# Attention decoder kernel: where a bias table is built, where a weight load is issued and where one projection group stands in the first block

## The chip, the cores and the metric

The kernel runs on one core of a Trainium2 chip. The metric is device time in microseconds (us) for one launch, the median of three runs; before the change it is 2969.03 us (2966.66 to 2971.7). All arithmetic is float32[...].

## The reference, cut to what matters

The program is one encoder layer on a short context (2 sequences of 77 rows), followed by one decoder layer on a long sequence (2 x 2048 rows, width 512, 16 heads of 32). The part that the change touches is the decoder's causal self-attention and, beside it, the encoder that is worked through in its gaps.

```python
def _rel_bias(emb, qlen, klen):
    rp = k - q
    bucket = jnp.where(rp < 0, jnp.minimum(-rp, MD - 1), jnp.minimum(rp, MD - 1) + MD)
    return emb[bucket].transpose(2, 0, 1)

# decoder, D = 512, H = 16, MD = 128, Tt = 2048
sb = _rel_bias(dec_rel_self, Tt, Tt) + causal[None]
yn = _ln(y, dec_n1_s, dec_n1_b)
y = y + _mha(yn, yn, dec_sa_in_w, dec_sa_in_b, dec_sa_out_w, dec_sa_out_b, sb)
y = y + _mha(_ln(y, ...), memory, ..., cb)      # cross-attention to the encoder's output
y = y + relu(ln(y) @ ff1 + b) @ ff2 + b
```

Scores are scaled by 1/sqrt(32), the bias is added, softmax is taken over the keys at or before the query.

## The kernel before, in words

The decoder's rows are cut into 8 blocks of 512 rows (2 sequences x 4), and a block into 4 row tiles t of 128. Heads are taken in 4 groups g of 4. A **unit** is one (block, group, row tile): 128 units in all, 16 in each block. The order of everything is written out by hand: `slot(n)` runs before unit n's turn of work, first the functions in `light[n]`, then the projection jobs in `jobs[n]`. Around a slot, `scores` writes q times k into PSUM and its copies with bias and maximum go to VectorE (L362 without bias, L369 with it, L376 the maximum), `exps` runs the exponentials on ScalarE (L379), `turn` transposes probabilities on TensorE (L403) and copies them out (L407 VectorE, L409 ScalarE), `values` multiplies them by v (L420). [...]

**The start (L921 to L960).** Four row tiles of x are loaded, `vecs` (scales and biases) and `rel` (the relative-bias embedding, 16 heads x 255) after them, then the first q and k weights (`wqk`, two buffers in `small_w`, L190) and the v weights (`wbig`, L196). `make_bias(1, rel, v)` (L88 to L94) writes a shifted copy of the self-attention table on VectorE in three instructions (L89 memset, L90 subtract, L93 memset of the causal part) and stores it 32 times into the DRAM tensor `tz` with one DMA (L94). Two rows of biases follow (`bv`, `bo`, L83). `load_bias` (L321) later reads `tz` back with a skew, four DMAs for each group. Then comes a software-pipelined layer norm over the four row tiles: `norm_stats` (L264, L265, L267 on VectorE and a power on GpSimd, L268), `norm_center` (L274) and `norm_turn` (L286 transposes on TensorE, evicted by one VectorE instruction at L293 and three ScalarE instructions at L291), with idle transposes (`warm`, L950) between them on TensorE. The result nT feeds the q and k projections (L206, L217), whose evictions are L208 (VectorE) and L222 (ScalarE).

**The stages of the encoder (L444 to L707)** are put one into each slot (`light[n]`): stage 5 multiplies by v (L529) and loads two more weights, stage 6 computes the scores of the first sequence (L538) and works on them on VectorE (L547 to L549). `light[1]` and `light[6]` also make the encoder's and the cross-attention's bias tables with the same `make_bias`.

**The jobs.** In the first block q and k of group 0 run at slot -1, of group 1 at slots 2 and 3, of group 2 at 4 and 5, of group 3 at 5 and 6. `load_next` issues weight loads ahead of the jobs, in the order of the jobs; it is called before every job and holds at most two small weights in flight, because there are two buffers:

```python
        def load_next():

            while len(loaded) < min(len(queue), ran[0] + (5 if ran[0] < 4 else 3)):
                ahead = [queue[i][2] for i in range(ran[0], len(loaded) + 1)]
                if sum(ahead) > 2:
                    break
                loaded.append(queue[len(loaded)][0]())
```

All DMAs are issued by SyncE's queue (SP), in program order: an issue that waits for a buffer holds up all later ones. TensorE, VectorE and ScalarE also run in program order. The tail of the program (cross-attention and the feed-forward of all blocks, in a form with seven products instead of eight) is not touched by the change, except for its line numbers, which move by up to three.

Of the kernel before, what the change touches and what calls it, by code (L numbers as in the profile page):

```python
# [54 lines left out]
def tile_encoder_decoder(ctx: ExitStack, tc: tile.TileContext, ins, out):  # L55
    nc = tc.nc
    x, src = ins["x"], ins["ctx_1024"]
# [19 lines left out]
    def vec(name, i):  # L77
        c = _COL[name] + i
        return vecs[:, c : c + 1]

    def row_into(t, name):
        i = _ROWS.index(name)
        nc.sync.dma_start(t, ins["rows"][i : i + 1, :].to_broadcast([P, D]))  # L83
# [4 lines left out]
    def make_bias(m, rel, v):  # L88
        nc.vector.memset(v[:, m, :], 0.0)  # L89
        nc.vector.tensor_scalar(v[:, m, P : P + NREL], rel[:, m, :], rel[:, m, 0:1], None, ALU.subtract)  # L90
        if m == 1:

            nc.vector.memset(v[:, m, 2 * P : LT], NEG)  # L93
        nc.sync.dma_start(tz[m][:, :RB, :], v[:, m : m + 1, :].to_broadcast([H, RB, LT]))  # L94
# [54 lines left out]
    with (  # L149
# [20 lines left out]
        def bank():  # L170

            i = count["bank"] % count["banks"]
            count["bank"] += 1
            return psum[:, i, :]
# [13 lines left out]
        def small_w(c0, name="dec_sa_in_wT"):  # L188
            w = sb.tile([P, NC, P], F32, name="wqk", tag="wqk", bufs=2)
            nc.sync.dma_start(w, wchunk(name, c0, P))  # L190
            return w
# [10 lines left out]
        def q_job(b, m, g):  # L202
            def run(w):
                mm = bank()
                for c in range(NC):
                    nc.tensor.matmul(mm, w[:, c, :], nTs[b, m][:, c, :], start=(c == 0), stop=(c == NC - 1))  # L206
                q = sb.tile([P, MB], F32, name="q", tag="q", bufs=3)
                nc.vector.tensor_scalar(q, mm, vec("dec_sa_in_b", g), SCALE, ALU.add, ALU.mult)  # L208
                qTs[b, m, g] = q

            return lambda: small_w(g * P), run, True

        def k_job(b, m, g):
            def run(w):
                mm = bank()
                for c in range(NC):
                    nc.tensor.matmul(mm, w[:, c, :], nTs[b, m][:, c, :], start=(c == 0), stop=(c == NC - 1))  # L217
                d, bi = kT[:, g, ts(m, MB)], vec("dec_sa_in_b", NC + g)
                if m >= 2:
                    nc.vector.tensor_scalar(d, mm, bi, None, ALU.add)  # L220
                else:
                    nc.scalar.activation(d, mm, AF.Identity, bias=bi)  # L222

            return lambda: small_w(D + g * P), run, True

        def v_job(b, m, t):
            def run(w):
                mm = bank()
                for c in range(NC):
                    nc.tensor.matmul(  # L230
                        mm, nTs[b, m][:, c, ts(t, P)], w[:, c, :], start=(c == 0), stop=(c == NC - 1)
                    )
                nc.vector.tensor_tensor(vv[:, m * TB + t, :], mm, bv, ALU.add)

            return lambda: big_w("v", b, m), run, False

        def out_job(b, m, t):
            def run(w):
                x1 = xr.pop((b, m, t))
                mm = bank()  # L240
                for c in range(NC):
                    nc.tensor.matmul(
                        mm, ots[b, m, c][:, ts(t, P)], w[:, c, :], start=(c == 0), stop=(c == NC - 1)
                    )
                nc.vector.tensor_tensor(x1, mm, x1, ALU.add)
                nc.sync.dma_start(y1[b][m][:, t, :], x1)

            return lambda: big_w("o", b, m), run, False

        def residual(b, m, t):  # L250
            x1 = xr[b, m, t] = sb.tile([P, D], F32, name="xr", tag="xr", bufs=2)
            nc.sync.dma_start(x1, x_rows[b, m, :, t, :])
            nc.gpsimd.tensor_tensor(x1, x1, bo, ALU.add)  # L253

        def norm_load(b, m, t, place=None):
            x1 = sb.tile([P, D], F32, name="xt", tag="xt", bufs=2) if place is None else place
            nc.sync.dma_start(x1, x_rows[b, m, :, t, :])
            xs[b, m, t] = x1

        def norm_stats(b, m, t):  # L260
            x1 = xs[b, m, t]
            st = sm.tile([P, 6], F32, name="bnst", tag="bnst")
            mv = sm.tile([P, 2], F32, name="bnmv", tag="bnmv")
            nc.vector.bn_stats(st, x1)  # L264
            nc.vector.bn_aggr(mv, st)  # L265
            rs = sm.tile([P, 2], F32, name="rstd", tag="rstd")
            nc.vector.tensor_scalar_add(rs[:, 0:1], mv[:, 1:2], EPS)  # L267
            nc.gpsimd.tensor_tensor(rs[:, 1:2], rs[:, 0:1], mhalf[:, 0:1], ALU.pow)  # L268
            xs[b, m, t] = x1, mv, rs

        def norm_center(b, m, t):
            x1, mv, rs = xs[b, m, t]
            xs[b, m, t] = x1
            nc.vector.tensor_scalar(x1, x1, mv[:, 0:1], rs[:, 1:2], ALU.subtract, ALU.mult)  # L274
# [608 lines left out]
        jobs = {n: [] for n in range(-1, len(units) + NU)}  # L883
# [4 lines left out]
        for x, (b, m) in enumerate(blocks):  # L888
            u = x * NU
            first = m == 0  # L890

            jobs[u + 1 if first else max(u - 3, -1)].append(v_job(b, m, 0))
            jobs[u + 2 if first else u - 2].append(v_job(b, m, 1))
            jobs[u + 3 if first else u + 1].append(v_job(b, m, 2))
            jobs[u + 4 if first else u + 2].append(v_job(b, m, 3))
            jobs[max(u - 5, -1)].append(q_job(b, m, 0))
            jobs[max(u - 4, -1)].append(k_job(b, m, 0))
            jobs[u - 1 if x else 2].append(q_job(b, m, 1))
            jobs[u if x else 3].append(k_job(b, m, 1))
            for g, at in ((2, 3), (3, 5)) if x else ((2, 4), (3, 5)):  # L900
                jobs[u + at].append(q_job(b, m, g))
                jobs[u + at + 1].append(k_job(b, m, g))
            for t in range(TB):
                end = x == len(blocks) - 1
                jobs[u + NU + (2 if end else 7) + t].append(out_job(b, m, t))
                at = u + NU + ((-1, 0, 3, 4)[t] if end else 6 + t)
                light[at].append(lambda b=b, m=m, t=t: residual(b, m, t))
                if x:
                    light[u - NU + 5 + t].append(lambda b=b, m=m, t=t: norm_load(b, m, t))
                    ahead[u - NU + 6 + t].append(lambda b=b, m=m, t=t: norm_stats(b, m, t))  # L910
                    light[u - NU + 6 + t].append(lambda b=b, m=m, t=t: norm_center(b, m, t))
                    light[u - NU + 7 + t].append(lambda b=b, m=m, t=t: norm_turn(b, m, t))
            for g in range(NC):
                d = divide(b, m, g)
                for k in range(2):
                    light[u + g * TB + TB + k].append(lambda d=d: next(d, None))
                at = u + g * TB - 3
                light[max(at, -1)].append(lambda b=b, m=m, g=g: load_bias(b, m, g))
# [7 lines left out]
        rel = pp[:H, 12288 : 12288 + 3 * NREL].rearrange("h (m u) -> h m u", u=NREL)  # L926
# [4 lines left out]
# [7 lines that stand above are left out]
# [1 line left out]
        ran = [0]  # L939
        load_next()  # L940
        v = pp[:H, 13056 : 13056 + 3 * LT].rearrange("h (m u) -> h m u", u=LT)
        make_bias(1, rel, v)
        row_into(bv, "sa_bv")
        row_into(bo, "dec_sa_out_b")

# [7 lines left out]
        for t in range(TB + 2):  # L953
            if t < TB:
                norm_stats(0, 0, t)
            if 1 <= t <= TB:
                norm_center(0, 0, t - 1)
            if t >= 2:
                norm_turn(0, 0, t - 2, apart=True)
                warm(6)  # L960
# [4 lines left out]
        def slot(n):  # L965
            for f in light[n]:
                f()
            for _, run, _ in jobs[n]:
                load_next()
                run(loaded[ran[0]])  # L970
                ran[0] += 1

        for r, fs in first_cross().items():
            light[len(units) // 2 + 1 + r] += fs
# [253 lines left out]
        turned_to, scored_to, at = {n: 0 for n in range(end)}, {}, [0]  # L1228
# [19 lines left out]
        while i < len(stream):  # L1248
            n = stream[i][0]
# [86 lines left out]
```

## Time and profile before

| | |
|---|---|
| median of 3 runs | 2969.03 us (2966.66 to 2971.7) |
| the profiled execution | 2966.73 us, span 2965.0 us, mean granted TensorE clock 0.986 |
| TensorE matmuls | 2878.4 us busy (97%) |
| VectorE | 2199.0 us busy (74%) |
| ScalarE | 1219.4 us busy (41%) |
| GpSimd | 738.0 us busy (25%) |
| DMA | 137.10 MB, mean 46 GB/s |

The page gives busy time for each engine over the whole span. A busy share of 97% is an average: at single places TensorE waits for a DMA or for VectorE, and those places are found in the waits and in the timeline of a stretch. The view of stretches gives, for each stretch, the busy time of each engine, the granted TensorE clock ("PEclk", 1.00 is full) and the DMA share. In the waits, "A <- B" reads: A stood idle until B.

### The profile page before, as it was taken

The page shows a single profiled execution, that of the slowest core. Times are in us where ns is not written, and L with a number is a line of the kernel's source. Part 1 is how long each engine was busy: PE and PEld are TensorE (multiplying, and loading weights), DVE is VectorE, ACT ScalarE, POOL GpSimd, SP SyncE. Part 2 cuts the span into 40 slices and gives each one's busy share as a digit, 9 for nine tenths or more (in the row PEclk, how much of TensorE's full clock was granted, in tenths as well). Part 3 has the DMA queues.
Part 4 walks back from the last instruction along what each step waited for, and adds up shares of the span by engine and source line. Part 5 has one row for each costly group of instructions (what it writes and reads, how often), then busy time and mean ns, then how long its engine had stood idle before and what let it go on. Part 6 is the DMA issues. An engine that isn't in the chain of part 4 may idle for free. (4 is left out here: it accounts for less than half of the span.)

```text
span 2965.0 us, 60688 instructions
## 1 busy us (share of the span) xinstructions
PE 2878.4 (97%) x24440; PEld 2021.5 (68%) x24440; DVE 2199.0 (74%) x6171; ACT 1219.4 (41%) x2211; POOL 738.0 (25%) x601
## 2 busy tenths in 40 slices
PE   8899999999999999999999997999999899999999
PEld 5456666666666556566666674777777777777788
DVE  4767688878987788788878883767676766766765
ACT  3344456546665455555556671213131313131311
POOL 0100000000000101000000004464646464646465
PEclk9799999999999999999999998999999999999999
DMA  6313301201112403202101224000001000000000
GB/s 174 87 53 116 102 16 51 66 16 44 33 41 70 128 19 87 65 23 63 39 16 37 64 75 136 1 29 1 29 1 38 10 29 1 29 1 29 1 15 15
DMA packets 117644, 137.10 MB, mean 46 GB/s; under 512 B 18241, under 2 KB 73073, under 8 KB 117235
## 3 DMA queue, kind: packets, MB, share of 16 engines
q1 hardware_dynamic: 117362, 133.22, 15.6%
q8 instruction: 192, 3.15, 0.5%
q14 instruction: 90, 0.73, 0.1%
HBM read 111.33 MB, written 21.86 MB: 45 GB/s over the span
## 5 line engine op out<-in xcount | busy, mean ns | idle before, releaser
L379 ACT ACTIVATE pp<-pp,nm 128x128 f32<-128x128 f32 (+15 forms) x512 | 614.0, 1209 | 201.4 <-DVE nm L376 198.8
L362 DVE TENSOR_SCALAR_CACHE_REDUCE pp<-psum 128x512 f32<-128x512 f32 (+3 forms) x1024 | 558.1, 589 | 47.3 <-PE psum L353 45.3
L403 PE MATMUL psum<-ident,pp 128*128 128x128 f32 x4352 | 549.5, 279 | 18.3 <-DVE mx L369 11.8
L403 PEld LDWEIGHTS psum<-ident,pp 128*128 128x128 f32 x4352 | 475.0, 142 | 132.3 <-DVE pp L362 57.1
L409 ACT COPY pts<-psum 128x512 f32<-128x512 f32 (+3 forms) x592 | 298.9, 577 | 510.3 <-PE psum L403 401.0
L1103 POOL TENSOR_TENSOR vv<-pp 128x512 f32<-128x512 f32 x320 | 416.7, 1318 | 148.0 <-PE psum L1120 122.8
L407 DVE COPY pts<-psum 128x512 f32<-128x512 f32 (+2 forms) x544 | 329.9, 660 | 42.0 <-PE psum L403 39.3
L353 PE MATMUL psum<-kT,q 32*128 32x512 f32 (+3 forms) x2560 | 352.0, 580 | 4.8 <-ACT kT L222 1.6
L420 PEld LDWEIGHTS psum<-pts,vv 128*32 128x32 f32 x8704 | 226.2, 110 | 124.0 <-issue 116.9
L420 PE MATMUL psum<-pts,vv 128*32 128x128 f32 x8704 | 278.7, 275 | 0.1
L268 POOL TENSOR_TENSOR rstd<-rstd,mhalf 128x1 f32<-128x1 f32 x32 | 18.2, 568 | 929.6 <-DVE rstd L267 929.6
L1140 ACT ACTIVATE kT<-kT,vecs 128x256 f32<-128x256 f32 x256 | 115.2, 499 | 297.5 <-DVE kT L1137 297.5
L1137 DVE TENSOR_TENSOR kT<-kT,psum 128x512 f32<-128x512 f32 x256 | 166.5, 680 | 86.7 <-PE psum L1120 81.5
L369 DVE CUSTOM_DVE_ANT_0 pp<-psum,bias 128x256 f32<-128x256 f32 (+1 forms) x512 | 209.6, 409 | 21.1 <-PE psum L353 21.1
L353 PEld LDWEIGHTS psum<-kT,q 32*128 32x128 f32 x2560 | 119.5, 184 | 148.5 <-issue 98.5
L1151 PE MATMUL psum<-vv 128*128 128x256 f32 x768 | 176.9, 381 | 0.0
L1120 PE MATMUL psum<-oT,vv 128*128 128x256 f32 x736 | 166.5, 380 | 0.0
L1151 PEld LDWEIGHTS psum<-vv 128*128 128x128 f32 x768 | 143.1, 190 | 26.8 <-issue 9.5
L1120 PEld LDWEIGHTS psum<-oT,vv 128*128 128x128 f32 x736 | 138.8, 190 | 24.4 <-issue 6.2
L1103 DVE TENSOR_TENSOR vv<-kT 128x512 f32<-128x512 f32 x160 | 137.8, 879 | 10.8 <-PE psum L1151 9.9
L253 POOL TENSOR_TENSOR xr<-xr,row_dec_sa_out_b 128x512 f32<-128x512 f32 x32 | 40.6, 1270 | 399.1 <-DMA xr<-in_x_dram 203.7
L206 PE MATMUL psum<-nT,wqk 128*128 128x512 f32 x256 | 120.3, 614 | 3.7 <-DMA wqk<-in_dec_sa_in_wT_dram 3.7
(175 smaller groups left out, 3928.6 us busy)
## 6 DMA issues: line engine op xcount, KB each, us to landing
wqk<-in_dec_sa_in_wT_dram SPq DMA_DIRECT2D x64, 256.0 KB, 3.6
bias<-tz SPq DMA_DIRECT2D x128, 128.0 KB, 3.8
wbig<-in_dec_sa_in_wT_dram SPq DMA_DIRECT2D x8, 1024.0 KB, 7.5
vv<-in_enc_ff_wT_dram SPq DMA_DIRECT2D x8, 1024.0 KB, 5.4
wbig<-in_dec_sa_out_wT_dram SPq DMA_DIRECT2D x8, 1024.0 KB, 7.4
xr<-in_x_dram SPq DMA_DIRECT2D x32, 256.0 KB, 3.3
y<-xr SPq DMA_DIRECT2D x32, 256.0 KB, 2.8
vv<-y SPq DMA_DIRECT2D x32, 256.0 KB, 3.4
```

The costliest lines, as they stand in the source:

```text
L353: nc.tensor.matmul(banks[r][:, : kn * P], q[rows4(r), ts(t, P)], kT[rows4(r), g, k0 * P : (k0 + kn) * P], start=True, stop=True,)
L362: nc.vector.tensor_scalar(p[:, k0 * P : (k0 + far) * P], s[:, : far * P], 1.0, None, ALU.mult, ALU.max, accum_out=st["mx"][:, r, c : c + 1],)
L369: nc.vector.tensor_tensor_reduce(p[:, (i + 1) * P - w : (i + 1) * P], s[:, far * P : kn * P], biases[b, m, g][:, r, 2 * P - w :], 1.0, LOW ...
L379: nc.scalar.activation(p, p, AF.Exp, bias=nm, accum_out=to)
L403: nc.tensor.transpose(pt[:, ts(x, P)], state[n]["p"][r][:, ts(k, P)], ident)
L407: nc.vector.tensor_copy(pts[:, : len(load), :], pt[:, :w])
L409: nc.scalar.copy(pts[:, : len(load), :], pt[:, :w])
L420: nc.tensor.matmul(ot[rows4(r), t, :], vv[:, k, ts(g * HC + r, HD)], got.pop((n, k, r)), start=(k == 0), stop=(k == i),)
L1103: engine.tensor_tensor(dst, quarter(*parts[0], n), quarter(*parts[2], n), SIGN[parts[1]])
L1120: nc.tensor.matmul(mm[:, ts(f, TOK)], a[:, c, ts(f, P)], b[:, c, :], start=(c == 0), stop=(c == 1))
L1137: nc.vector.tensor_tensor(dst, dst, got, SIGN[sign])
L1151: nc.tensor.matmul(mm[:, t, :], lhs[:, c, ts(t, P)], rhs[:, c, :], start=(n == 0 and c == 0), stop=(n == 3 and c == 1),)
```

## The change

It moves three things in the start and the first block.

1. `make_bias(1, rel, v)` is no longer called before the two bias rows are loaded and before the first layer norm, but inside the loop over the row tiles, at t = 3, after the statistics of tile 3 and the centering of tile 2.
2. In the first block, the job q of group 3 moves from slot 5 to slot 6, ahead of k of group 3, which stays there. For the other blocks the slots are the same as before, written in another way.
3. After slot 5, `load_next()` is called once more, so that the weights of k of group 3 are asked for there.

```diff
-            for g, at in ((2, 3), (3, 5)) if x else ((2, 4), (3, 5)):
+            for g, at, then in ((2, 3, 4), (3, 5, 6)) if x else ((2, 4, 5), (3, 6, 6)):
                 jobs[u + at].append(q_job(b, m, g))
-                jobs[u + at + 1].append(k_job(b, m, g))
+                jobs[u + then].append(k_job(b, m, g))
...
         v = pp[:H, 13056 : 13056 + 3 * LT].rearrange("h (m u) -> h m u", u=LT)
-        make_bias(1, rel, v)
         row_into(bv, "sa_bv")
         row_into(bo, "dec_sa_out_b")
...
                 norm_center(0, 0, t - 1)
+            if t == 3:
+                make_bias(1, rel, v)
             if t >= 2:
                 norm_turn(0, 0, t - 2, apart=True)
...
                 run(loaded[ran[0]])
                 ran[0] += 1
+            if n == 5:
+                load_next()
```

The number of instructions on each engine is the same. On SP only one issue changes its place: the store of `tz` (L94) goes behind the two bias rows (L83). On TensorE q of group 3 (L206) goes behind the scores, values and transposes of units 6, 4 and 5 and the encoder's scores (L353, L420, L403, L538). On VectorE the three instructions of `make_bias` go behind L274 of row tile 2, and the eviction of q of group 3 (L208) goes behind the encoder's softmax work and the third table.

## The prediction

> **What bounds the kernel now.** I read the busy shares first, then the waits and the timeline of the two places that the diff touches (0 to 30 us and 83 to 110 us), then the stretches around them.
>
> ```profile
> PE 2878.4 (97%) x24440; PEld 2021.5 (68%) x24440; DVE 2199.0 (74%) x6171; ACT 1219.4 (41%) x2211; POOL 738.0 (25%) x601
> ```
>
> TensorE is the bound as an average. The change moves no work off it, so it can only gain where TensorE and VectorE both stand still. The waits of 0 to 30 us:
>
> ```profile
> DVE pp L90 <- DMA pp<-in_rel_dram: 6.4, 1, 6.4
> DVE pp L369 <- PE psum L353: 4.5, 1, 4.5
> ...
> SPq L321 <- DMA tz<-pp: 1.1, 1, 1.1
> ```
>
> The timeline there:
>
> ```profile
> 7.61 0.34 DVE L90 TENSOR_SCALAR pp<-pp 16x255 f32<-16x255 f32 x1 [6.37 <-DMA pp<-in_rel_dram]
> 8.03 0.17 DVE L93 MEMSET pp<- 16x128 f32 x1
> 8.13 0.62 DVE L264 BATCH_NORM_STATS2 bnst<-xt 128x6 f32<-128x512 f32 x1
> 8.23 0.33 SPq L94 DMA_DIRECT2D tz<-pp  x1
> ...
> 16.77 3.60 PE L206 MATMUL psum<-nT,wqk 128*128 128x512 f32 x8
> ...
> 18.19 1.75 SPq L321 DMA_DIRECT2D bias<-tz  x4
> ...
> 24.58 0.93 PE L353 MATMUL psum<-kT,q 32*128 32x128 f32 x14 [0.78 <-ACT kT L222]
> 25.64 0.29 DVE L369 CUSTOM_DVE_ANT_0 pp<-psum,bias 128x128 f32<-128x128 f32 x1 [4.48 <-PE psum L353]
> ```
>
> VectorE stands until 7.61 for the embedding table and all statistics queue behind it. But two chains meet at 25.64. One is x, norm, q, k, scores. The other is table, store to DRAM (8.23), four loads back (18.19 to 19.94, lags 5.4 to 6.0 us in the DMA view, so the last lands at about 25.5), first biased score. The wait at L369 is put down to the scores, yet the score matmuls started 1.06 us before it; at the same spot of group 1 VectorE follows after 0.5 us (59.53, 60.05). So here the table landed last, by about half a us.
>
> The second place:
>
> ```profile
> PE psum L206 <- DMA wqk<-in_dec_sa_in_wT_dram: 3.7, 1, 3.7
> ```
>
> ```profile
> 90.45 6.52 PE L206 MATMUL psum<-nT,wqk 128*128 128x512 f32 x8 [3.69 <-DMA wqk<-in_dec_sa_in_wT_dram]
> 96.90 0.93 PE L353 MATMUL psum<-kT,q 32*128 32x384 f32 x8
> ...
> 102.66 5.40 PE L217 MATMUL psum<-nT,wqk 128*128 128x512 f32 x8
> 107.99 1.14 PE L353 MATMUL psum<-kT,q 32*128 32x512 f32 x8
> ```
>
> ```profile
> 97.01 0.75 DVE L208 TENSOR_SCALAR q<-psum,vecs 128x512 f32<-128x512 f32 x1 [12.95 <-PE psum L206]
> 97.85 0.29 DVE L362 TENSOR_SCALAR_CACHE_REDUCE pp<-psum 128x128 f32<-128x128 f32 x1
> ...
> 109.30 0.41 DVE L362 TENSOR_SCALAR_CACHE_REDUCE pp<-psum 128x256 f32<-128x256 f32 x1
> ```
>
> ```profile
> 86.80:90.45 3.65, 0.00 (x0) 0.03 (x1) 0.00 (x0) 0.69 (x1) 0.00 (x0) 0.85 1.07 327
> 90.45:96.97 6.52, 6.52 (x12) 2.57 (x12) 0.00 (x0) 0.00 (x0) 0.00 (x0) 0.56 0.09 29
> ```
>
> TensorE waits 3.69 us for the weights of q3 (q of group 3), then runs at a granted clock of 0.56, 6.52 us for what takes 3.60 elsewhere. VectorE idles 12.95 us. From 97 to 140 us VectorE is the bound (5.31 of 5.76, 5.27 of 5.34, then 9.69 of 10 us at 130 to 140), so an earlier start of VectorE at 97 carries through.
>
> **The change part by part.** The sum is made against the profiled execution (2966.73 us, span 2965.0, so 1.7 around it), which lies 2.3 under the median of 2969.03.
>
> *Bias table later.* Statistics start with x tile 0 (issued 0.74, lag 2.7: 3.4) instead of 8.13; tile 1 (1.65 + 3.9 = 5.6) sets the pace. From the start of tile 1's statistics (9.07 before, 5.67 after) the loop took 4.8 us to the end of tile 2's centering (13.86), behind which the table now stands: 10.5 us. The table's three instructions (0.38 + 0.34 + 0.17 and gaps) make 1.0 us, so L93 ends near 11.4 and the store is issued there, 3.2 us later than 8.23. The last turn is ready near 13.2 instead of 16.0, q starts near 13.9 and the scores at 21.8 instead of 24.58. Projection weights (issued 3.5 to 4.6) keep their place, and the v weights (4.56 + 7.8 = 12.4) come long before use.
>
> The other chain decides. The same store alone on the queue, at 109.40, took 9.5 us to land (DMA view; its stretch moves 96 to 98 GB/s). On SP it is now behind the two bias rows (256 KB each), which it no longer blocks: the second one's issue took 4.11 us behind the table, the context's 3.76. The rows now go out at about 5 to 6 us and drain behind the v weights by about 12.4, when the store's first packets could come anyway. The context's issue stays behind the store. Landing: 11.4 + 9.5 = 20.9 (18.2 before). The four loads back took 7.3 us before, with rows and context still draining; quiet groups show 2.7 to 2.9 lag plus 1.3 between first and last issue. I take 5.1 between these: 26.0 against 25.5, **+0.5 us**. Bounds: a store as quick as before and quiet loads give 19.8 + 4.2 = 24.0 (-1.5); 21.2 + 7.3 = 28.5 (+3.0). So the 2.8 us that the first chain wins are waited away at L369. Behind it on VectorE everything queues, and TensorE waits for exponentials at L403.
>
> [...] Row: 768 KB in 9.5 us. [...] The trace has the very transfer, so 9.5 stands. [...] Row: after the gap before 28.3 the v matmuls took 5.20 instead of 3.60 at clock 0.51. The gap now grows from about 3 to 5 us (21.0 to 26.5). [...] I take 0 and keep 1.7 for the range.
>
> *q3 a slot later, k3's load asked for in slot 5.* The issue order on SP around these loads is unchanged: q3's weights at 84.46 (lag 5.9: 90.3), k3's at 86.8, when k of group 2 releases the buffer, then x. So no queue is passed. The extra `load_next` only keeps k3's load from following slot 6's issues. On TensorE the scores of unit 6 now follow k of group 2 at 86.7 instead of 96.90. VectorE starts at 87.2 instead of 97.85, 10.65 earlier. The same work up to the third table took 11.45 to 109.30; with L208 (0.75) now inside it, the scores of unit 7 could be taken at 99.4. TensorE: the encoder's scores end 4.85 after VectorE's start, 92.05; q3's weights are there (90.3, margin 1.7). q3 and k3 then take 2 x 3.43 at full clock, 98.9, or about 100.7 with one half-rate window, as k3 had before (5.40). Half a us later VectorE goes on: 99.4 to 101.2 instead of 109.30, 8.1 to 9.9 earlier. Since that stretch always has gaps, I take the slow end: **-8.3 us**. k3's weights, the transfer behind q3's, are needed at 95.5. What is late next: the third table's store (109.40, landed at 118.9) and behind it row tile 2 of block 1, whose statistics VectorE takes at 122.51, 3.6 us later. The store starts about 10.6 us earlier, the statistics only 8 to 10, so the cover grows; without it each us of lag would come straight off the gain.
>
> *The other blocks* keep their slots, and the rest of the program only moves in time. Sum: +0.5 - 8.3 = -7.8: 2958.9 for the profiled execution, **2961 us** for the median.
>
> **The rivals.**
> 1. *The start gives back more.* The bias lands at 28.5 (+3.0) and a further half-rate window costs 1.7, with the weights' gain at its low end, -6.6 (the 3.69 wait and 6.52 - 3.60 = 2.9 of slow clock, and nothing for VectorE): -1.9, so 2967. For: all of it sits on one DMA chain with 0.5 us to spare. Against: rows no longer drain ahead of the loads back. Chance 0.22 for results of this kind.
> 2. *Slower: the loads back are held up.* The next weights and 3 MB of encoder weights now follow the four loads at once, as TensorE is already through with q and k. If the engines do not serve them in order, the loads may lag as group 1's did among that stream (11.75 us for its second): 20.9 + 1.3 + 11.75 = 34.0, +8.5, plus 1.7 of clock, minus 8.3: 2971. It decides from a bias landing after about 33.8; over 0.2% slower needs 39.7. Against: group 1's were issued after that stream. Chance 0.09.
> 3. *The store does not matter.* [...] Chance 0.1; the trace's row speaks against it.
>
> My forecast has the rest, 0.59.
>
> **How the numbers follow.** The three runs spread over 5 us and 0.2% is 5.9 us, about what a measurement of this kernel can tell from no change; faster means below 2963.1. The likeliest case holds 2958.5 to 2963.5; with the third rival and most of the first the range is 2956 to 2968. Faster: nearly all of the likeliest and the third case and little of the first, 0.68. Slower by over 0.2% (above 2975): half of the second, 0.05. Same: 0.27.
>
> **What would show it.** Right: no wait of TensorE on `wqk` near 86 us, the scores of unit 6 directly after k of group 2, VectorE's idle time there under 5 us instead of 12.95, the scores of unit 7 some 8 us earlier; the table's store issued near 11.4 and landing near 21, the first L369 at 25 to 28 with TensorE waiting since about 22. Wrong: the first L369 near 22 (the table was never the bound), or beyond 30; or a wait on `wqk` that stands again before q3 or k3.

## The result and the profile after

The changed kernel takes 2960.87 us (median of 14 runs, 2956.82 to 2962.97). The kernel before takes 2967.25 us (14 runs, 2960.14 to 2971.7). The ratio is 0.998, with a 95% interval of 0.9972 to 0.9989; the medians are 6.4 us apart. The profiled execution took 2961.12 us, its span is 2959.3 us and its mean granted clock 0.987. Its busy line is nearly that of before, with the same number of matmuls. TensorE is 3.1 us less busy; two jobs alone, q and k of group 3, took 11.92 us and now take 9.00, with less of them at a slow clock (granted 0.56 at q3 and 0.68 at k3 before, 0.68 and 1.00 now).

```profile
PE 2875.3 (97%) x24440; PEld 2018.0 (68%) x24440; DVE 2205.4 (75%) x6171; ACT 1220.9 (41%) x2211; POOL 735.6 (25%) x601
```

**The start.** The waits of 0 to 30 us have no line for `in_rel_dram` any more, and the wait of L369 is now put down to the table:

```profile
DVE pp L369 <- DMA bias<-tz: 7.5, 1, 7.5
```

The timeline of the start (start, duration, engine, line, operation, number of records; in brackets the idle time before it and what ended it; a q or k job's four matmuls stand as eight records, x8):

```profile
3.45 0.69 DVE L264 BATCH_NORM_STATS2 bnst<-xt 128x6 f32<-128x512 f32 x1 [3.45 <-DMA xt<-in_x_dram]
...
5.95 0.69 DVE L264 BATCH_NORM_STATS2 bnst<-xt 128x6 f32<-128x512 f32 x1 [1.40 <-DMA xt<-in_x_dram]
...
11.60 0.17 DVE L93 MEMSET pp<- 16x128 f32 x1
11.79 0.33 SPq L94 DMA_DIRECT2D tz<-pp  x1
...
13.69 3.60 PE L206 MATMUL psum<-nT,wqk 128*128 128x512 f32 x8
...
21.32 1.74 SPq L321 DMA_DIRECT2D bias<-tz  x4
21.50 0.93 PE L353 MATMUL psum<-kT,q 32*128 32x128 f32 x14 [0.78 <-ACT kT L222]
25.59 0.29 DVE L369 CUSTOM_DVE_ANT_0 pp<-psum,bias 128x128 f32<-128x128 f32 x1 [7.51 <-DMA bias<-tz]
```

The statistics start 4.7 us earlier (3.45 in place of 8.13), q 3.1 us earlier (13.69, before 16.77), the scores too (21.50, before 24.58). The store is issued 3.6 us later and is read back from 21.32. So VectorE starts on the first biased score at 25.59, before at 25.64: TensorE's whole lead is waited away.

**The first block.** The timeline from 83 to 105 us:

```profile
85.05 2.71 SPq L190 DMA_DIRECT2D wqk<-in_dec_sa_in_wT_dram  x2
87.29 0.93 PE L353 MATMUL psum<-kT,q 32*128 32x384 f32 x8
...
88.23 0.29 DVE L362 TENSOR_SCALAR_CACHE_REDUCE pp<-psum 128x128 f32<-128x128 f32 x1 [3.59 <-PE psum L353]
...
93.04 5.40 PE L206 MATMUL psum<-nT,wqk 128*128 128x512 f32 x8
...
98.27 3.60 PE L217 MATMUL psum<-nT,wqk 128*128 128x512 f32 x8
...
99.78 0.33 SPq L94 DMA_DIRECT2D tz<-pp  x1
...
101.80 1.14 PE L353 MATMUL psum<-kT,q 32*128 32x512 f32 x8
...
102.96 0.42 DVE L362 TENSOR_SCALAR_CACHE_REDUCE pp<-psum 128x256 f32<-128x256 f32 x1 [2.54 <-PE psum L353]
```

TensorE no longer waits for `wqk`. The scores of unit 6 follow k of group 2 directly, and the weights of q3 (q of group 3), which are asked for at 85.05, arrive in time behind other work. VectorE's idle time of 12.95 us is now 3.59 before unit 6 and 2.54 before unit 7. Unit 6 starts on VectorE 9.6 us earlier (97.85 to 88.23), unit 7 6.3 us earlier (109.30 to 102.96). That lead is still 6.3 us at unit 48 and 5.8 at unit 127, the last of the self-attention.

The stretches (length, then busy time of TensorE, weight loads, VectorE, ScalarE and GpSimd; then granted clock, DMA share, GB/s) show the clock at the v matmuls of the start and at q3:

```profile
25.60:32.60 7.00, 6.65 (x11) 3.00 (x12) 6.51 (x34) 4.31 (x18) 1.36 (x2) 0.51 0.99 327
...
93.00:98.40 5.40, 5.40 (x11) 2.34 (x10) 5.31 (x7) 0.00 (x0) 2.62 (x2) 0.68 0.01 3
98.40:102.00 3.60, 3.60 (x13) 1.41 (x15) 1.96 (x4) 0.09 (x1) 0.00 (x0) 1.00 0.33 39
```

In the kernel before, the slow stretch at the v matmuls was this one:

```profile
28.00:31.40 3.40, 3.40 (x5) 1.65 (x6) 3.16 (x15) 2.50 (x10) 0.55 (x1) 0.51 1.02 389
```

### The profile page after: what moved, and what is told of

The parts are those of the page before. It is cut to its first block, busy times and chain, and to the rows that moved or that the text cites. A ratio compares the mean times of both kernels' runs of the same rounds, so it can differ in the third digit from the quotient of the medians.

```text
span 2959.3 us, 60687 instructions
## 1 busy us (share of the span) xinstructions
PE 2875.3 (97%) x24440; PEld 2018.0 (68%) x24440; DVE 2205.4 (75%) x6171; ACT 1220.9 (41%) x2211; POOL 735.6 (25%) x601
## 5 line engine op out<-in xcount | busy, mean ns | idle before, releaser
L403 PE MATMUL psum<-ident,pp 128*128 128x128 f32 x4352 | 549.1, 279 | 18.0 <-DVE mx L369 11.8
L403 PEld LDWEIGHTS psum<-ident,pp 128*128 128x128 f32 x4352 | 474.8, 142 | 132.2 <-DVE pp L362 57.1
L353 PE MATMUL psum<-kT,q 32*128 32x512 f32 (+3 forms) x2560 | 354.1, 579 | 7.6 <-DVE mx L369 3.5
L420 PEld LDWEIGHTS psum<-pts,vv 128*32 128x32 f32 x8704 | 226.2, 110 | 123.9 <-issue 116.9
L420 PE MATMUL psum<-pts,vv 128*32 128x128 f32 x8704 | 278.9, 276 | 0.0
L369 DVE CUSTOM_DVE_ANT_0 pp<-psum,bias 128x256 f32<-128x256 f32 (+1 forms) x512 | 209.8, 410 | 24.1 <-PE psum L353 16.6
L353 PEld LDWEIGHTS psum<-kT,q 32*128 32x128 f32 x2560 | 119.7, 184 | 152.4 <-issue 99.4
L230 PE MATMUL psum<-wbig,nT 128*128 128x512 f32 x256 | 118.6, 607 | 0.6 <-DVE mx L369 0.3
```

Source lines behind the costliest of these rows:

```text
L353: nc.tensor.matmul(banks[r][:, : kn * P], q[rows4(r), ts(t, P)], kT[rows4(r), g, k0 * P : (k0 + kn) * P], start=True, stop=True,)
L369: nc.vector.tensor_tensor_reduce(p[:, (i + 1) * P - w : (i + 1) * P], s[:, far * P : kn * P], biases[b, m, g][:, r, 2 * P - w :], 1.0, LOW ...
L403: nc.tensor.transpose(pt[:, ts(x, P)], state[n]["p"][r][:, ts(k, P)], ident)
L420: nc.tensor.matmul(ot[rows4(r), t, :], vv[:, k, ts(g * HC + r, HD)], got.pop((n, k, r)), start=(k == 0), stop=(k == i),)
```

## The experiments

Line numbers of kernels that add lines to `make_bias` are three higher (split store) or five higher (wide store) from there on. "Before" is the kernel before, run on the same chip as the experiment; experiments on different chips are compared by their ratios. "First biased score" is the first L369.

### The parts apart

**Only the table moved** (q3 back in slot 5, no extra load):

```diff
-            ... else ((2, 4, 5), (3, 6, 6)):
+            ... else ((2, 4, 5), (3, 5, 6)):
...
-            if n == 5:
-                load_next()
```

> The bias table is made late as in the changed kernel, but q of group 3 stays in slot 5 and the extra weight request is gone. My theory: the table's chain (store, loads back) ends at the same moment as before (25.5 us), so this part is worth nothing: first biased score at 25.3 to 25.9 us, median within 1 us of the kernel before, at most +0.6 us from a longer half-rate stretch of TensorE; TensorE waits for wqk near 87 us for about 3.7 us again. Rival (both parts give about half): 3 us below the kernel before. Rival (the late table costs): 2 us or more above it.

Measured: 2966.09 us (11 runs), before 2965.57 (22 runs), ratio 1.0004 (0.9995 to 1.0013).

```profile
25.46 0.29 DVE L369 CUSTOM_DVE_ANT_0 pp<-psum,bias 128x128 f32<-128x128 f32 x1 [7.81 <-DMA bias<-tz]
...
90.84 6.73 PE L206 MATMUL psum<-nT,wqk 128*128 128x512 f32 x8 [3.77 <-DMA wqk<-in_dec_sa_in_wT_dram]
```

The first biased score stands where it stood, and the old wait for q3's weights is back. This part alone is worth nothing that can be told: the interval reaches from 1.5 us less to 3.9 us more.

**Only the group moved and its load asked for early** (the table where it was before):

```diff
         v = pp[:H, 13056 : 13056 + 3 * LT].rearrange("h (m u) -> h m u", u=LT)
+        make_bias(1, rel, v)
...
-            if t == 3:
-                make_bias(1, rel, v)
```

> The table is made at its old place; q of group 3 stands in slot 6 and its partner's weights are asked for after slot 5. My theory: all of the gain is here: scores of unit 6 near 86.7 us instead of 96.9, everything from unit 7 on 6.3 to 7 us earlier, median 6 to 7 us below the kernel before, equal to or 0.6 us below the changed kernel. Rival (half each): 3 us below the kernel before.

Measured: 2959.04 us (8 runs), ratio 0.9975 (0.9965 to 0.9985). So the gain is here, as far as the intervals can tell.

```profile
24.79 1.57 PE L353 MATMUL psum<-kT,q 32*128 32x128 f32 x16 [0.78 <-ACT kT L222]
25.31 0.29 DVE L369 CUSTOM_DVE_ANT_0 pp<-psum,bias 128x128 f32<-128x128 f32 x1 [3.94 <-PE psum L353]
...
91.92 3.70 PE L206 MATMUL psum<-nT,wqk 128*128 128x512 f32 x8
95.46 3.60 PE L217 MATMUL psum<-nT,wqk 128*128 128x512 f32 x8
...
100.14 0.42 DVE L362 TENSOR_SCALAR_CACHE_REDUCE pp<-psum 128x256 f32<-128x256 f32 x1 [0.85 <-PE psum L353]
```

In this execution q3 took 3.70 us in place of 5.40 at a granted clock of 0.68 in the changed kernel, and VectorE waited 0.85 us before unit 7 in place of 2.54. The 1.7 us between the two are the clock's. Its start is that of the kernel before, yet here the loads back had landed at 24.50 and the first biased score follows the scores by 0.52 us. So before the change the two chains of the start end within about 1 us of each other, and either can be the last.

**The group moved, its load not asked for early**:

```diff
-            if n == 5:
-                load_next()
```

> The changed kernel without the extra weight request after slot 5. The load for k of group 3 is then issued behind the store of the third table on SP. My theory: that store takes 9.5 us to land from about 99.8, so the weights come at about 110.5 instead of 92; TensorE waits at k of group 3 from 98.3 for about 12 us and runs at half rate after it, the scores of unit 7 come at about 114 to 116 instead of 101.8: 11 to 14 us above the changed kernel, 5 to 8 above the kernel before. Rival (the request is idle, since the weights would be there anyway): same time as the changed kernel.

Measured: 2973.68 us (8 runs), ratio 1.0029 (1.0019 to 1.0039), slower than before.

```profile
100.31 0.32 SPq L94 DMA_DIRECT2D tz<-pp  x1
100.73 4.81 SPq L190 DMA_DIRECT2D wqk<-in_dec_sa_in_wT_dram  x2
...
110.81 5.91 PE L217 MATMUL psum<-nT,wqk 128*128 128x512 f32 x8 [13.54 <-DMA wqk<-in_dec_sa_in_wT_dram]
```

Without the request in slot 5, the load of k3 (k of group 3) is issued behind the third table's store, and TensorE waits 13.54 us for it. Unit 7's first maximum comes at 118.62, in the changed kernel at 103.77. The one line `load_next()` is therefore worth some 14 us (by the ratios 1.0029 and 0.998 it is 0.0049 x 2967 = 14.5): without it the moved group loses.

**k3 one slot later still** (slot 7):

```diff
-            ... else ((2, 4, 5), (3, 6, 6)):
+            ... else ((2, 4, 5), (3, 6, 7)):
```

> The changed kernel with k of group 3 in slot 7 instead of slot 6, so that only q stands in front of the scores of unit 7. My theory: in the changed kernel VectorE stands 2.54 us before unit 7 because TensorE works off q and k there; with k moved VectorE goes on without a wait: unit 7's first biased maximum at 101.2 instead of 103.8, and k runs in slot 7 where VectorE is the bound: 2 to 2.6 us below the changed kernel. Rival (the gain is capped by VectorE or returns at slot 7): same time as the changed kernel.

Measured: 2954.52 us (5 runs, 2953.74 to 2958.65), ratio 0.9964 (0.9951 to 0.9976).

```profile
97.61 1.14 PE L353 MATMUL psum<-kT,q 32*128 32x512 f32 x8
...
99.66 0.40 DVE L362 TENSOR_SCALAR_CACHE_REDUCE pp<-psum 128x256 f32<-128x256 f32 x1
...
105.57 5.33 PE L217 MATMUL psum<-nT,wqk 128*128 128x512 f32 x8
```

VectorE's wait before unit 7 is gone (no bracket), and k3 runs beside VectorE's work. This version is 11.1 us under before (2965.57), and by the ratios some 5 us under the changed kernel (0.0016 x 2967 = 4.7), though the two intervals still touch; on the same chip it is 4.5 us under the kernel with only the group moved. The place itself gives what was expected: from unit 5 to unit 7 it wins 2.6 us over the changed kernel's profile. Most of the rest of its lead in the profile is the clock of this one execution: 0.7 us at the v matmuls of the start (4.69 us in place of 5.83) and 2.1 us between units 40 and 60 (last section).

### What the start waits for

**The store first on the queue** (`rel` loaded second, the table made after tile 0's statistics, the store ahead of the v weights and the two rows):

```diff
...
+        norm_stats(0, 0, 0)
+        make_bias(1, rel, v)
         load_next()
...
         row_into(bv, "sa_bv")
         row_into(bo, "dec_sa_out_b")
...
```

> The changed kernel, with the embedding table loaded second on SP, the bias table made right after the first tile's statistics, and its store issued ahead of the v weights and the bias rows. My theory: the store goes out near 6 us instead of 11.8 and lands near 16.5 to 18 behind the q and k weights, the loads back end at 21 to 22.5 instead of 25.5; the scores are ready at about 21.5 to 22, so the first biased score starts at 22 to 22.7: 2.8 to 3.6 us below the changed kernel (2957 to 2958 where that takes 2961). Rival (the table's chain is not what holds the start): first biased score still after 25 us, same time.

Measured: 2959.51 us (5 runs), before 2968.71, ratio 0.9966 (0.9954 to 0.9979). The first biased score did not come earlier.

```profile
5.66 0.34 SPq L94 DMA_DIRECT2D tz<-pp  x1
...
6.57 4.31 SPq L83 DMA_DIRECT2D row_sa_bv<-in_rows_dram  x1
10.93 3.47 SPq L83 DMA_DIRECT2D row_dec_sa_out_b<-in_rows_dram  x1
...
15.58 1.76 SPq L321 DMA_DIRECT2D bias<-tz  x4
...
26.05 0.29 DVE L369 CUSTOM_DVE_ANT_0 pp<-psum,bias 128x128 f32<-128x128 f32 x1 [9.02 <-DMA bias<-tz]
```

The store lands 5.7 us earlier, but the loads back then take 8.1 to 9.0 us to land instead of 2.4 to 2.8. In the 8 us after their issue the queue moves 265 GB/s, some 2.1 MB, of which the four loads are 0.5 MB; the v weights and the rows were issued just ahead of them (the issues of the rows take 4.31 and 3.47 us). The first biased score stays at 26, as the rival said, though for another reason: the table's chain still holds the start, by its loads back. The ratio lies below that of the changed kernel (0.998), as does that of the next experiment on the same chip. The intervals overlap, and the changed kernel was not timed on that chip, so no gain over it is shown.

**A quarter of the store** (only the four heads of group 0 at the new place, the other twelve behind the first loads back):

```diff
-        nc.sync.dma_start(tz[m][:, :RB, :], v[:, m : m + 1, :].to_broadcast([H, RB, LT]))
+        store_bias(m, v, 0, HC if m == 1 else H)
...
+        light[-1].append(lambda: store_bias(1, v, HC, H))
```

> The changed kernel, but only the four heads of group 0 (192 of 768 KB) are stored at the table's new place; the other twelve heads are stored after the loads back for group 0. My theory: the store's 9.5 us are its amount at about 98 GB/s; a quarter lands about 4 us after its issue (15.5 to 16.5), the loads back end at about 20 to 20.5, ahead of the scores, and the first biased score starts 0.5 us after the score matmuls, at 22 instead of 25.6, without a wait on the bias DMA: 3 to 4 us below the changed kernel. Rival (a fixed cost of the store, not its amount): the quarter takes over 7 us, first biased score at 24 or later, under 1.5 us gained.

Measured: 2958.25 us (6 runs), ratio 0.9966 (0.9953 to 0.9978).

```profile
11.26 0.32 SPq L97 DMA_DIRECT2D tz<-pp  x1
...
20.78 1.74 SPq L324 DMA_DIRECT2D bias<-tz  x4
...
25.08 0.29 DVE L372 CUSTOM_DVE_ANT_0 pp<-psum,bias 128x128 f32<-128x128 f32 x1 [7.53 <-DMA bias<-tz]
```

The stretch from 14 to 20 us, here and in the changed kernel:

```profile
14.00:20.00 6.00, 6.00 (x15) 2.47 (x13) 0.75 (x1) 0.00 (x0) 0.00 (x0) 1.00 0.23 29
14.00:20.00 6.00, 6.00 (x15) 2.66 (x14) 0.75 (x1) 0.40 (x2) 0.00 (x0) 1.00 0.88 97
```

SP issues the loads back as soon as the store has landed (in the changed kernel it waits 8.6 us for it), so the gap between the two SP rows is the store's time: 9.52 us for 192 KB, 9.53 for 768 KB in the changed kernel. The DMA share of 0.23, against 0.88, says that on average about a quarter as much of the 16 engines was at work, for just as long. In these two runs the total amount did not set the store's time. The first biased score comes only 0.5 us earlier (25.08): my theory fell, and what the rival said of the store and the start came true.

**Wider rows** (four copies of the table side by side, so that each partition sends 8 rows of 6144 B in place of 32 of 1536 B):

```diff
+            wide = vv[:H, 8:11, :].rearrange("h a d -> h (a d)").rearrange("h (o u) -> h o u", o=1)
+            nc.vector.tensor_copy(wide.rearrange("h o (a t) -> h (o a) t", t=LT), v[:, m : m + 1, :].to_broadcast([H, 4, LT]))
+            nc.sync.dma_start(tz[m][:, :RB, :].rearrange("h (b a) t -> h b (a t)", a=4), wide.to_broadcast([H, RB // 4, 4 * LT]))
```

> The self-attention table is written four times side by side by one more VectorE copy (into columns of vv that are free then), and its store to DRAM reads rows of 6144 B, 8 for each of 16 partitions, in place of 32 rows of 1536 B; the same 768 KB go to the same places. All else as in the changed kernel. Where 768 KB from 16 partitions and 192 KB from 4 partitions both took 9.5 us, each partition sent 32 rows of 1536 B. Theory A, the time goes with the number of rows for each partition: 8 rows in place of 32, the store lands 3 to 5 us after its issue; its issue is some 1 to 1.5 us later for the copy (about 13.1), it lands at 16 to 18, the four loads back are no longer held up by it, the scores (about 22.5, as the copy also delays the last centering) decide, the first L369 near 22.5 to 23.5 in place of 25.59, and the whole some 2 to 3 us shorter, 2958 to 2959. Theory B, it goes with the bytes for each partition (48 KB): still 9.5 us, landing at 22.6, the first L369 near 26.9, and the whole 1 us longer, about 2962.

Measured: 2958.08 us (10 runs), before 2966.25, ratio 0.9973 (0.9964 to 0.9983).

```profile
12.21 0.33 SPq L97 DMA_DIRECT2D tz<-vv  x1
...
21.28 1.74 SPq L326 DMA_DIRECT2D bias<-tz  x4
```

9.07 us, for a quarter of the rows. Theory A (rows) falls; theory B (bytes for each partition) foresaw the landing within 1.3 us. Its first biased score was expected at 26.9 and came at 25.49. Its total, about 2962, did not come: the measured total is the one that theory A named, but without theory A's early landing.

**Half the rows** (each table stored 16 times, each load back made of eight DMAs):

```diff
-RB = 32
+RB = 16
```

> The tables are stored 16 times in place of 32 (RB 16), and every load back is made of eight DMAs of 16 rows in place of four of 32. All else as in the changed kernel. The first store then moves 384 KB, 24 KB from each of the 16 partitions. Theory B, left by the two runs before (the time goes with the bytes that each partition sends; 48 KB took 9.5 us with 1536 B rows and about 9 us with 6144 B rows): it lands about 5.5 us after its issue, at 17.3; eight issues of 0.45 us bring the last load back out at 20.5 and its landing to about 23.5, so the first L369 is near 23.7 in place of 25.59. The whole is up to 2 us shorter, 2958 to 2960, unless the doubled number of issues of later bias tiles holds up weight loads on SP. Rival, that a store from 16 partitions has a fixed time: it lands at 21, the eight loads land at 26.5 to 27.5, and the whole is 1 to 2 us longer, 2962.

Measured: 2959.0 us (10 runs, 2953.97 to 2961.01), before 2966.01, ratio 0.998 (0.9969 to 0.999).

```profile
10.96 0.33 SPq L94 DMA_DIRECT2D tz<-pp  x1
...
16.52 3.59 SPq L321 DMA_DIRECT2D bias<-tz  x8
...
22.34 0.29 DVE L369 CUSTOM_DVE_ANT_0 pp<-psum,bias 128x128 f32<-128x128 f32 x1 [5.10 <-DMA bias<-tz]
```

Half the bytes for each partition, and the store takes 5.56 us. The first biased score comes 3.25 us earlier than in the changed kernel, and still waits for the bias. Theory B had put the store's landing at 17.3 and the first biased score at 23.7; they came at 16.52 and 22.34, and the total lies inside the expected 2958 to 2960. So the store is what the start waits for, and in these runs its time goes with the bytes that each partition sends:

| kernel | store | for each partition | time |
|---|---|---|---|
| changed kernel | 768 KB, 16 partitions | 32 x 1536 B = 48 KB | 9.53 us |
| a quarter | 192 KB, 4 partitions | 32 x 1536 B = 48 KB | 9.52 us |
| wider rows | 768 KB, 16 partitions | 8 x 6144 B = 48 KB | 9.07 us |
| half the rows | 384 KB, 16 partitions | 16 x 1536 B = 24 KB | 5.56 us |

Other executions agree: in other kernels the same stores took 9.47 to 9.89 us (768 KB, four kernels), 9.25 (a quarter), 9.08 (wider rows) and 5.44 (half the rows). The last row against the first gives, as an estimate from two points, about 4 us for 24 KB, 6 GB/s for a partition, and 1.6 us beside it. What sets this rate is not shown.

**A warm TensorE in the gap** (26 idle transposes between the scores of units 0 and 1):

```diff
+            for _ in range(26):
+                nc.tensor.transpose(psum[:, 7, :P], ident, ident)
```

> The changed kernel with 26 idle transposes on TensorE between the scores of units 0 and 1, where it waits for the bias table (about 22 to 25 us). My theory: the gap no longer drops the clock; the first v matmuls take 3.6 to 3.7 us instead of 5.83, and the scores of unit 2 start up to 0.6 us earlier (unit 2's first maximum at 35.1 instead of 35.7, as in the kernel before), not the full 2.2 us, since VectorE is busy until 34. Rival (the half rate costs its full length): unit 2 two us earlier.

Measured: 2963.83 us, one run.

```profile
28.89 3.70 PE L230 MATMUL psum<-wbig,nT 128*128 128x512 f32 x8
```

The v matmuls take 3.70 us (5.83 in the changed kernel, at a granted clock of 0.63 from 28.25 to 34.10), but the total shows no gain. The loads back landed later in this execution, and the first biased score came at 26.23 in place of 25.59; unit 2's first maximum (L376) came at 35.55, before that 35.73, so it made up 0.8 us on the way. A single run cannot tell 1 us in the total; what VectorE hides of the slow clock is worked out below from all profiles.

### Putting gains together

> The split store together with k of group 3 in slot 7. My theory: the two gains lie on different waits and add: 3 to 4 from the start and 2.5 to 6 from slot 7 below the changed kernel, median 2949 to 2955 where the changed kernel takes 2961. Rival (one wait hides the other): no faster than the better of the two alone.

> The store of e9 and k of group 3 in slot 7 as in e4. If both gains hold and lie in different places, 2 to 3 us under e4: about 2952, by theory A; by theory B as e4 or 1 us above it, 2955.

> The halved store of e11 with k of group 3 in slot 7 as in e4. If the gains add: about 2952.5 to 2953.5, 1 to 2 us under e4's 2954.5. If the start gains nothing after the v matmuls, or if eight issues hold up the first block's weight loads, 2954 to 2957.

| k3 in slot 7 with | median us | runs | ratio to before |
|---|---|---|---|
| nothing else | 2954.52 | 5 | 0.9964 (0.9951 to 0.9976) |
| a quarter of the store | 2955.01 | 5 | 0.9953 (0.9940 to 0.9965) |
| wider rows | 2954.73 | 5 | 0.9961 (0.9949 to 0.9974) |
| half the rows | 2954.04 | 5 | 0.9962 (0.9949 to 0.9976) |

None of them can be told from k3 in slot 7 alone: in all three it was the second case that came, not the sum. For half the rows the timeline shows one place where its earlier start is spent:

```profile
97.62 0.40 DVE L362 TENSOR_SCALAR_CACHE_REDUCE pp<-psum 128x256 f32<-128x256 f32 x1
...
103.95 6.14 PE L217 MATMUL psum<-nT,wqk 128*128 128x512 f32 x8
110.02 0.50 PE L353 MATMUL psum<-kT,q 32*128 32x128 f32 x8
```

Unit 7 starts 2.0 us earlier than with k3 in slot 7 alone (97.62 against 99.66), but k3 takes 6.14 us (5.33 there; in the changed kernel 3.60 at a granted clock of 1.00), the scores of unit 8 wait for it, and they start at 110.02 against 110.83 (0.8 us earlier).

## Why the prediction was right, step by step

- **The table's chain decides the start: right.** Predicted: store issued at 11.4, landed at 20.9, scores ready at 21.8, first biased score 0.5 us later than before. Measured: 11.79, 21.3, 21.50, and 0.05 us earlier, which is no difference: the same start gave 25.46 to 25.83 in four kernels (only the table moved, the change, k3 in slot 7, no early load). The loads back took 4.15 us from the first issue to the last landing in place of 5.1: that small term was too high. The lower bound was not sound: a store "as quick as before" was put at 8.4 us (19.8 less 11.4), but the rows of before, 8.23 to 18.19, say 9.96. My reading that the table came last by half a us before the change fits the profile of the kernel with only the group moved, where the loads back landed 1 us earlier and the scores decided. The 9.5 us for the store, read from the third table's, were right (9.53 measured), and the third rival fell with that. The range's lower end, 2956, counted on that rival too; no run shows a store of 768 KB that lands early: it took 9.07 to 9.96 us in the kernels told of here. With half the rows the first biased score does move, by 3.25 us, which shows the chain; with only the table moved the total does not move, so this change gave the start nothing that can be told.
- **The slow clock taken at nothing: off by 0.6 us.** The v matmuls took 5.83 us in place of 5.20, and unit 2 came 0.59 us later than before although the first biased score did not. No run shows the 1.7 us that I kept for the range, and that the first two rivals add for the clock, as lost at the v matmuls. What the rows show is a granted clock of 0.51 over 7.00 us (25.60 to 32.60) where it was 3.40 us (28.00 to 31.40). But most of what was added fell ahead of the v matmuls, which start at 28.25, so they lost 0.63 us. The profiles of all kernels together show how far VectorE's cover goes. From the first unit's to the third unit's maximum (L376) it takes 8.98 us with v matmuls of 3.70 us (only the group moved) and still 8.98 with 4.69 (k3 in slot 7), 9.17 with 5.20 (before), 9.80 with 5.83 (the change), 10.10 with 6.13 (no early load) and 10.32 with 6.35 (half the rows, k3 in slot 7). The other eight profiles lie on the same line. So in these profiles v matmuls of up to about 5 us cost nothing, and beyond that each us costs one. The row of before (5.20 us) stood at the edge of the cover; to take the clock at nothing was to put it well inside. The sum of the start, +0.5, is near the measured +0.59, but by other terms (bias 0.0, clock +0.6): that is luck. And the +0.6 is one execution's: with the same code up to there the v matmuls took 5.83, 5.68, 6.13 and 4.69 us with the late table (the change, only the table moved, no early load, k3 in slot 7) and 5.20 and 3.70 with the early one.
- **The group's gain: right in mechanism, 8.3 us was too much.** At unit 7 the change is -6.33 us; without the 0.59 of the start it is -6.9. The slow end of my own range was 8.1 (109.30 - 101.2); the 8.3 that went into the sum does not come out of it. Of the 1.2 us that are left, two terms were mis-sized. I let VectorE follow the scores after 0.5 us, by a row of group 1; the rows at the very spot, 96.90 to 97.85 and 107.99 to 109.30, stood among those that I showed, and say 0.95 and 1.31. After the change it is 0.94 and 1.16, so 0.4 us was lost at unit 6 and 0.7 at unit 7. The rest held: the encoder's scores end 4.81 us after VectorE's start (4.85 predicted), q3 and k3 take 8.76 us with one slow stretch (8.65). Where no slow clock falls on q3 (only the group moved, a quarter of the store, half the rows), units 5 to 7 gain 8.6 us; the fast end of the range was 9.9, too much by 1.3, about the same two delays.
- **The early load: its price was missing.** The prediction said that it "only keeps k3's load from following slot 6's issues" and gave no number. Slot 6 issues the third table's store, which takes 9.5 us, and without the early load TensorE waits 13.54 us, more than the whole gain. A step costed at nothing should have had its own bound here.
- **The third table's cover: right.** Its store is issued at 99.78 instead of 109.40, earlier by more than unit 7 is. It lands about 109.3, and the statistics of row tile 2 follow at 116.18 without a wait, 6.9 us later (3.6 before). The lead of 6.3 us stays until unit 48.
- **The rivals.** The bias landed neither at 28.5 (first) nor late enough to show (second): the four loads back were served in 2.4 to 2.8 us although the next weights and the encoder's followed at once. Where the bulk was issued ahead of them, with the store first on the queue, they took 8.1 to 9.0 us.
- **The total.** I predicted -7.8 us on the profiled execution; its time fell by 5.6 (2966.73 to 2961.12), the median by 6.4. That the predicted 2961.0 meets the measured 2960.87 so closely is partly luck: the three runs of before (2969.03) lay 1.8 us above its median of 14 runs, which made up for the 1.4 to 2.2 us by which the sum was too large.

## What to carry to other kernels

Where two chains meet at one instruction, winning on one of them is worth only what the other has to spare (here 0.05 us of the 3.1 by which TensorE was earlier): move the later one, or leave both. Before a weight load changes its place, read what is issued on the same queue between its old and its new place; one long store there can cost more than the whole move brings (here a wait of 13.54 us, against a gain of 6.4). For the delay between two engines take the row at the very spot, with that tile's shape, not one from a quieter place (here 0.95 and 1.31 us, against 0.5).

## What was not expected of the hardware

- The broadcast store from 16 partitions (9.53 us) was no faster when only 4 of them sent (9.52), and little faster with rows four times as wide (9.07); it was with half the bytes for each partition (5.56). In the changed kernel it showed a DMA share of 0.88 at 97 GB/s, while the v matmuls' stretch moved 327 GB/s at 0.99: here a high share did not mean a high throughput.
- Some slow stretches of the granted clock fall at the same work in one profiled execution and not in another. Far behind the change, the changed kernel's has two of them:

```profile
640.00:670.00 30.00, 29.10 (x277) 19.39 (x274) 23.93 (x80) 14.26 (x22) 0.00 (x0) 0.89 0.04 10
1510.00:1530.00 20.00, 19.67 (x156) 12.00 (x150) 15.00 (x51) 8.37 (x10) 0.00 (x0) 0.83 0.01 1
```

The one of the kernel with half the rows, whose code differs there only in the number of loads for a bias, has neither:

```profile
640.00:670.00 30.00, 29.50 (x315) 17.71 (x314) 26.89 (x93) 16.34 (x21) 0.00 (x0) 1.00 0.01 2
1510.00:1530.00 20.00, 19.83 (x203) 12.04 (x205) 17.47 (x62) 15.77 (x20) 0.00 (x0) 1.00 0.01 2
```

Nor has the one of the kernel with a quarter of the store, whose code there is the same (clock 1.00 in both stretches). Units 40 to 60 take 342.3 to 343.0 us in the eight profiles with the first of them and 340.7 to 340.9 in the six without, so one such stretch is worth about 2 us. Others stay: a mean clock below 1 in the stretch from 1770 to 1800 us stands in all fourteen (0.77 before and after the change). With one profile for each kernel, chance and the kernel's own timing cannot be told apart here; but executions of one kernel differ in their mean clock too (before, on one chip: 2960.05 us at a mean clock of 0.988, 2970.64 at 0.984).

The profiled execution of the kernel with half the rows, 2953.97 us, was the fastest of ten with a median of 2959.0. What the 3.25 us that half the rows win at the start are worth at the end therefore stays open. In the profile 3.0 us of them are left at unit 2, and the lead at unit 40 is 4.7 us (1.7 of it the clock at q3), while the ratios to before, 0.998 for both kernels, do not differ.
